# First attention: scores three groups ahead of their exponentials, banks handed out in another order, pieces of work moved between visits

## The chip, the core and the metric

The kernel runs on one core of a Trainium2 chip. The core has five engines, each with its own instruction queue that is worked off in order: TensorE (PE, matmul; PEld is its weight load), VectorE (DVE), ScalarE (ACT), GpSimd (POOL) and SyncE (SP, which issues the DMAs). Matmuls write to PSUM, which has eight banks; a bank of the tiles used here holds 128 partitions of 2 x 256 floats. The metric is the device time of one execution in microseconds (us).

## The reference

A block of four layers, all in float32, on x of 16 batches x 256 tokens x 128 channels: attention a, a gated expert network, attention b, and the expert network again, each after a layer norm and with a residual. The change is in attention a alone. It has 16 heads of 8 channels, and `_binlinear` is a linear layer whose weights are sign(W) times the mean of |W| over a row. Cut to what it computes:

```python
x = x + _L0_attn_a_ref(_layernorm(x, axis=-1), ...)
x = x + _L0_ffn_ref(_layernorm(x, axis=-1), ...)
x = x + _L0_attn_b_ref(_layernorm(x, axis=-1), ...)
x = x + _L0_ffn_ref(_layernorm(x, axis=-1), ...)

def _L0_attn_a_ref(x, Wq, bq, Wk, bk, Wv, bv, Wp, bp):
    q = split_heads(_binlinear(x, Wq, bq))
    k = split_heads(_binlinear(x, Wk, bk))
    v = split_heads(_binlinear(x, Wv, bv))
    att = jnp.einsum('bhtd,bhsd->bhts', q, k) * scale
    att = jax.nn.softmax(att, axis=-1)
    y = jnp.einsum('bhts,bhsd->bhtd', att, v)
    y = y.transpose(0, 2, 1, 3).reshape(B, T, C)
    return _binlinear(y, Wp, bp)
```

## The kernel before

Attention a goes over 16 batches b, and in each over four groups g of four heads; a group has the number G = 4b + g, from 0 to 63. The four heads j of a group lie on partitions 32j to 32j + 31, so their matmuls use different quarters of PE's rows and run side by side.

Each group passes through these steps. `scores` (L395) computes q k' for a head: two matmuls of 256 columns into one bank (a_s), and a DVE reduce of the bank to the negative row maxima (a_nm, L406). `maxima` (L411) turns the maxima with two PE transposes into a bank (a_mx), and DVE adds them to q (a_qa, L421). `exponentials` (L423) computes k q' a second time, transposed and with the maximum taken off through a_qa, into a bank (a_t); ACT takes the exponential (a_pT, L435). `values` (L438) multiplies two groups' probabilities with v, 16 matmuls of 32 columns of weights into half a bank (a_mv), which ACT copies (a_oT, L454).

Around these, each batch has pieces: `channels` (L352) transposes the normalised x to a_xnT; `project` (L359) makes q and k (bank a_pqk), which ACT copies out with the bias (a_qkc, L367), and SP sends to DRAM by one DMA (a_qks) and back by four into the spread layout (a_qk); `project_v` (L381) makes v; `tokens` (L456) transposes the heads (bank a_oq), DVE takes reciprocals and multiplies (a_rs L471, a_y L472); `turn_back` (L478) transposes again and DVE adds a bias (a_yT, L486); `project_out` (L491) makes the output, DVE adds it to x (L498), and `normalise` (L156) runs its statistics on DVE and the rest on POOL; `gate_channels` (L503) and `gate` (L510) make the logits that the expert network needs.

The order is written out by hand: all five engines run in the order of the program. The main loop (L579) goes over i. Its block issues scores of group i and exponentials of group i - 2, in two halves of two heads each; `together` (L520) takes turns between generators, so that PE's matmuls of four heads alternate. After the block `visit(i)` (L554) issues maxima of group i - 1, and the pieces that `table` (L547) gives to s = i mod 4 with a batch offset: first those that share the bank of the maxima, then those with a bank of their own, then those that share the bank of the values; values are issued for two groups at odd s, in visit i for groups i - 3 and i - 2. Project runs one batch ahead.

Every PSUM tile of attention a has one tag with eight buffers, so the banks go round in the order in which the tiles are asked for: s0, s1, t2, t3, s2, s3, t0, t1 in a block (s for scores, t for exponentials, with the head's number), then those of the visit (two or three), then the next block's.

`begin` (L283) is the start: five warming matmuls on zeros, batch 0's normalisation, the weights (`weights` L252 binarises two matrices on DVE and transposes them on PE; `keep` copies them out), and batch 0's q and k straight into the spread layout (L326). The weights of v and p are binarised in steps between these, and their transposes and copies come in visit 2 (L597). The last visits, from i = n + 2 (n = 64), take 20 pieces of the expert network's first matmuls in between (`own_at`, L578).

Of the kernel before, what the change touches and what calls it, by code (L numbers as in the profile page):

```python
# [17 lines left out]
P = 128  # L18
# [59 lines left out]
def hybrid_kernel(ctx: ExitStack, tc: tile.TileContext, io):  # L78
# [115 lines left out]
    def attention_a(place, filling):  # L194
# [4 lines left out]
        with ExitStack() as st:  # L199
# [4 lines left out]

            wT = {}
# [35 lines left out]
            def fills():  # L241

                for n in "qk":
                    wS[n] = pool.tile([P, NG, NJ, 32], F32, tag="sgn", name=f"wS_{n}")
                    nc.gpsimd.memset(wS[n], 0.0)
                for i in range(4):
                    nm = wpool.tile([P, 2, NJ, 32], F32, tag=f"nm{i}", name=f"a_nm{i}")
                    nc.gpsimd.memset(nm, 0.0)
                    nms.append(nm)
                values_tile()  # L250

            def weights(names, w):  # L252

                alpha = small.tile([P, 2], F32, tag="alpha", name=f"alpha_{names}")
                nc.vector.tensor_reduce(
                    alpha, w, AX.X, ALU.add, apply_absolute_value=True
                )
                nc.vector.tensor_scalar(alpha, alpha, 1.0 / C, None, ALU.mult)
                s = pool.tile([P, 2, C], F32, tag="sg", name=f"sgn_{names}")
                nc.vector.tensor_scalar(s, w, 0.0, 1.0, ALU.is_gt, ALU.subtract)  # L260
                nc.vector.scalar_tensor_tensor(s, w, 0.0, s, ALU.is_ge, ALU.add)
                yield

                nc.vector.tensor_tensor(s, s, w, ALU.subtract)
                nc.vector.tensor_tensor(s, s, w, ALU.add)
                yield
                nc.vector.tensor_tensor(
                    s, s, alpha.unsqueeze(2).to_broadcast([P, 2, C]), ALU.mult
                )
                pt = psum.tile([P, 2, T], F32, tag="x", name=f"wT_{names}", bufs=8)[:, :, 0:C]  # L270
                for i in range(2):
                    nc.tensor.transpose(pt[:, i, :], s[:, i, :], ident)
                yield pt
# [9 lines left out]
            def begin():  # L283


                fills()

                warm = psum.tile([P, 2, T], F32, tag="x", name="a_warm", bufs=8)
                for _ in range(5):
                    nc.tensor.matmul(  # L290
                        warm[:, 0], wS["q"][:, 0].rearrange("p j e -> p (j e)"),
                        wS["q"][:, 0:2].rearrange("p g j e -> p (g j e)"),
                        start=True, stop=True,
                    )
# [9 lines left out]
                together(channels(0, half_bank("a_lnT0")))  # L304
                next(qk)
                pt = next(qk)
                nc.vector.tensor_scalar(bq, a_bq, SCALE, None, ALU.mult)
                nc.vector.tensor_scalar(bq_, a_bq_, SCALE, None, ALU.mult)
                xns[1] = normalise(1)
# [6 lines left out]
                keep("qk", pt)  # L316
                vp = weights("vp", a_w[1])
                spread_tile(False)
                to = spread[0]
                q[0], k[0] = to[:, 0], to[:, 1]  # L320
                for half in range(2):
                    for i, (n, bias) in enumerate((("q", bq_), ("k", a_bk_))):
                        pp = psum.tile([P, 2, T], F32, tag="x", name=f"a_p{n}_{half}", bufs=8)
# [6 lines left out]
                        if i:  # L330
                            next(vp)
                        for j in range(2):
                            g = 2 * half + j
                            if i:
# [8 lines left out]
                return vp  # L343
# [5 lines left out]
            def half_bank(name):  # L349
                return psum.tile([P, 2, T], F32, tag="x", name=name, bufs=8)[:, 0]  # L350

            def channels(b, pt):  # L352
                for t in range(2):
                    nc.tensor.transpose(pt[:, t * P : (t + 1) * P], xns[b][:, t, :], ident)
                yield
                xnT[b] = pool.tile([P, T], F32, tag="xnT", name=f"a_xnT{b}")
                nc.scalar.copy(xnT[b], pt)

            def project(b):  # L359

                pp = psum.tile([P, 2, T], F32, tag="x", name=f"a_pqk{b}", bufs=8)
# [10 lines left out]
                to = spread[b % 3]  # L372
# [22 lines left out]
            def scores(G, j):  # L395
# [3 lines left out]
                sc = psum.tile([P, 2, T], F32, tag="x", name=f"a_s{G}_{j}", bufs=8)  # L399
# [23 lines left out]
            def exponentials(G, j):  # L423
# [3 lines left out]
                sc = psum.tile([P, 2, T], F32, tag="x", name=f"a_t{G}_{j}", bufs=8)  # L427
# [28 lines left out]
            def tokens(b):  # L456

                ys[b] = work.tile([P, 2, C], F32, tag="y", name=f"a_y{b}")
                po = psum.tile([P, 2, 2, P], F32, tag="x", name=f"a_oq{b}", bufs=8)
# [18 lines left out]
            def turn_back(b, py):  # L478
# [7 lines left out]
                nc.vector.tensor_scalar(yTs[b], py, a_bv, None, ALU.add)  # L486
# [40 lines left out]
            def of(b):  # L527
                return 0 <= b < NB
# [11 lines left out]
            vp = begin()  # L540
            for i in range(2):
                spread_tile(True)
                values_tile()
            nc.gpsimd.memset(ones, 1.0)
# [3 lines left out]
                ([(project, 1)], [(gate, -3)], []),  # L548
                ([], [(project_out, -2)], []),
                ([(tokens, -1)], [], [(project_v, 1), (channels, 2)]),  # L550
                ([], [(turn_back, -1)], [(gate_channels, -2)]),
            )

            def visit(i):  # L554
                b, s = divmod(i, NG)
                alone, with_maxima, with_values = (
                    [(f, b + d, *r) for f, d, *r in pieces if of(b + d)] for pieces in table[s]
                )
                own_bank = lambda which: psum.tile(
                    [P, 2, T], F32, tag="x", name=f"a_m{which}{i}", bufs=8  # L560
                )
                parts = []
                if 1 <= i < n + 1 or with_maxima:
                    pt = own_bank("x")
                    if 1 <= i < n + 1:
                        parts.append(maxima(i - 1, pt[:, 0]))
                    parts += [f(*r, pt[:, 1]) for f, *r in with_maxima]
                parts += [f(*r) for f, *r in alone]
                pair = s % 2 == 1 and 3 <= i < n + 2
                if pair or with_values:  # L570
                    pt = own_bank("v")
                    parts += [f(*r, pt[:, k]) for k, (f, *r) in enumerate(with_values)]
                    if pair:
                        parts.append(values(i - 3, pt[:, 1]))
# [3 lines left out]
            own_at = {2: 3, 3: 3, 4: 2, 5: 3, 6: 4, 7: 3, 8: 2}  # L578
            for i in range(NG * (NB + 2) + 1):  # L579
                b, s = divmod(i, NG)  # L580
                for half in range(2):
# [3 lines left out]
                    if 2 <= i < n + 2:  # L585
                        parts += [exponentials(i - 2, 2 - 2 * half + j) for j in range(2)]
                    together(*parts)
                    if not i and not half:
                        together(channels(1, half_bank("a_lnT1")))
                if i >= n + 2:  # L590
                    place["h"] = (epool, 5, psum, "x", 8)
                    place["y"] = (psum, "x", 8)
# [3 lines left out]
                if i == 2:  # L596
                    keep("vp", next(vp))  # L597
                    pv = psum.tile([P, 2, T], F32, tag="x", name="a_pv0", bufs=8)
                    together(project_v(0, pv[:, 0]))
                visit(i)  # L600
                if i == 1:
                    xns[2] = normalise(2)
                if i in (5, 9):
                    load_later(i // 9)
                if s == 3 and of(b + 3):
                    xns[b + 3] = normalise(b + 3)
# [423 lines left out]
    def bank(psum, tag, name, bufs):  # L1030

        if tag == "ss":
# [307 lines left out]
```

## Time and profile before

| | us |
|---|---|
| time, median of 3 runs (lowest to highest) | 1552.05 (1549.66 to 1553.44) |
| time of the profiled execution | 1550.1 |
| span of its trace | 1548.3 |
| start of group 0's scores, of group 4's scores | 14.07, 34.29 |
| twelve batches in the middle, each | 17.30 |
| first matmul of the expert network | 299.95 |
| granted PE clock, mean of the span | 0.997 |

The span is what the trace covers, from the first instruction to the last. A row of the windows view gives the length of a stretch, then for PE, PEld, DVE, ACT and POOL the busy time and, in brackets, the number of instructions, then the granted clock of PE as a share of full speed, the busy share of the DMA engines and their GB/s. A row of the timeline gives start, duration, engine, line, operation, output<-inputs and how many instructions were merged; a bracket at its end is idle time before it and what ended that. One float32 matmul stands in PE's rows as two records. Records of PE overlap: a matmul of 256 columns lasts 374 ns in its record, and the next in the same rows starts 216 ns after it.

### The profile page before, as it was taken

How to read it: one execution, taken by the hardware profiler on the slowest of the kernel's cores; microseconds unless marked ns; L12 is line 12 of the kernel's file. 1: busy time of each engine (PE TensorE's matmuls, PEld its weight loads, DVE VectorE, ACT ScalarE, POOL GpSimd, SP SyncE). 2: the span in 40 equal slices, each digit the busy share in tenths (PEclk: the TensorE clock that was granted, in tenths of full speed). 3: DMA queues.
4: the chain of work that ended last, by engine and by line, in shares of the span. 5: the costliest groups of instructions: out<-in, count | busy, mean ns of one | idle time of the engine just before them, and what ended most of it. 6: DMA issues, size and time to landing. Idle time of an engine off the chain costs nothing. (4 is left out here: it accounts for less than half of the span.)

```text
span 1548.3 us, 30874 instructions
## 1 busy us (share of the span) xinstructions
PE 1527.9 (99%) x12284; PEld 860.9 (56%) x12284; DVE 810.3 (52%) x1642; ACT 833.4 (54%) x2074; POOL 403.5 (26%) x518
## 2 busy tenths in 40 slices
PE   8999999999999999999999999999999999999998
PEld 5777777644444444444577777777544444444444
DVE  6888887536133312212599999999363133212122
ACT  3666666544443434343588888888644434344342
POOL 4232323100001000003289888887100000000000
PEclk8999999999999999999999999999999999999999
DMA  3511111000223211111122222222001133211210
GB/s 83 155 32 29 29 36 36 2 8 1 71 64 80 58 38 39 36 41 34 22 57 51 50 48 53 56 54 41 8 1 49 48 79 89 52 48 37 45 41 7
DMA packets 174127, 69.91 MB, mean 45 GB/s; under 512 B 74520, under 2 KB 173600, under 8 KB 173728
## 3 DMA queue, kind: packets, MB, share of 16 engines
q1 hardware_dynamic: 173408, 67.54, 19.1%
q8 instruction: 97, 1.59, 0.4%
q10 hardware_dynamic: 576, 0.41, 0.1%
q14 instruction: 46, 0.38, 0.1%
HBM read 50.88 MB, written 12.58 MB: 41 GB/s over the span
## 5 line engine op out<-in xcount | busy, mean ns | idle before, releaser
L1042 ACT ACTIVATE hT<-ph,head 128x512 f32<-128x512 f32 x512 | 351.2, 687 | 420.9 <-PE ph L1040 418.4
L1040 PE MATMUL ph<-xn,w 128*128 128x512 f32 x1024 | 464.5, 594 | 1.1 <-ACT hT L1042 1.1
L1051 PE MATMUL py<-hT,w 128*128 128x512 f32 (+1 forms) x1040 | 461.3, 586 | 1.0 <-ACT logits L941 0.5
L1051 PEld LDWEIGHTS py<-hT,w 128*128 128x128 f32 x1040 | 196.6, 190 | 237.3 <-issue 230.8
L1040 PEld LDWEIGHTS ph<-xn,w 128*128 128x128 f32 x1024 | 191.3, 190 | 228.0 <-issue 224.2
L1165 DVE SCALAR_TENSOR_TENSOR gy<-py,head,gb 128x512 f32<-128x512 f32 x82 | 61.5, 750 | 425.6 <-PE py L1051 419.3
L855 ACT ACTIVATE b_pr<-b_s,b_nm 128x256 f32<-128x256 f32 x512 | 235.9, 473 | 58.8 <-DVE b_nm L850 58.6
L406 DVE TENSOR_REDUCE a_nm<-a_s 128x2 f32<-128x512 f32 x256 | 160.3, 685 | 52.0 <-PE a_t L429 35.6
L850 DVE TENSOR_REDUCE b_nm<-b_s 128x4 f32<-128x1024 f32 x128 | 152.7, 1193 | 21.5 <-PE b_s L840 21.2
L840 PE MATMUL b_s<-b_kT,b_qd 64*64 64x256 f32 x1024 | 159.9, 382 | 0.2 <-ACT b_pr L855 0.2
L435 ACT ACTIVATE a_pT<-a_t 128x512 f32<-128x512 f32 x256 | 133.2, 598 | 47.2 <-PE a_t L429 46.7
L865 DVE STREAM_TRANSPOSE b_pT<-b_pr 128x1024 f32<-128x1024 f32 x128 | 157.1, 1227 | 0.0
L840 PE MATMUL b_s<-strip,b_qb 64*64 64x256 f32 x2048 | 156.6, 376 | 0.0
L840 PE MATMUL b_s<-b_kS,b_qd 64*64 64x256 f32 x1024 | 156.5, 382 | 0.0
L401 PE MATMUL a_s<-a_qk 32*128 32x256 f32 x1024 | 134.4, 390 | 0.0
L730 POOL TENSOR_TENSOR b_qd<-b_qsel,head 128x512 f32<-128x512 f32 x64 | 84.0, 1335 | 177.6 <-DMA b_qsel<-b_qT 168.9
L152 POOL TENSOR_SCALAR ve<-mv 128x2 f32<-128x2 f32 x64 | 14.6, 229 | 435.1 <-DVE mv L149 429.2
L429 PE MATMUL a_t<-a_qa,a_qk 32*128 32x256 f32 x1024 | 121.9, 394 | 3.5 <-DVE a_qa L421 2.7
L855 ACT ACTIVATION_READ_ACCUMULATOR b_pr<-b_s,b_nm 128x1 f32 x512 | 104.1, 203 | 0.0
L401 PEld LDWEIGHTS a_s<-a_qk 32*128 32x128 f32 x1024 | 91.1, 185 | 22.5 <-issue 15.2
L161 POOL TENSOR_SCALAR xn<-x,mv,rstd 128x128 f32<-128x128 f32 x126 | 99.7, 800 | 6.6
L840 PEld LDWEIGHTS b_s<-strip,b_qb 64*64 64x64 f32 x2048 | 78.3, 133 | 32.2
(176 smaller groups left out, 1439.7 us busy)
## 6 DMA issues: line engine op xcount, KB each, us to landing
gb<-gd SPq DMA_DIRECT2D x128, 256.0 KB
w<-in_w SPq DMA_DIRECT2D x2, 2048.0 KB
a_qks<-a_qkc SPq DMA_DIRECT2D x15, 256.0 KB
a_qk<-a_qks SPq DMA_DIRECT2D x60, 64.0 KB
x<-in_x SPq DMA_DIRECT2D x16, 128.0 KB
b_qs<-b_qT SPq DMA_DIRECT2D x64, 32.0 KB
b_qsel<-b_qT SPq DMA_DIRECT2D x64, 32.0 KB
b_z<-b_qs SPq DMA_DIRECT2D x16, 128.0 KB
```

What stands on the lines that cost most here:

```text
L161: (last or nc.gpsimd).tensor_scalar(xn[:, t, :], xs[b][:, t, :], mv[:, t, 0:1], rstd[:, t : t + 1], ALU.subtract, ALU.mult,)
L401: nc.tensor.matmul(sc[:, t, :], q[b][rows, g, t * P : (t + 1) * P], k[b][rows, g, :], start=True, stop=True,)
L406: nc.vector.tensor_reduce(nms[G % 4][:, :, j, 0:1].rearrange("p t o -> p (t o)"), sc, AX.X, ALU.max, negate=True,)
L429: nc.tensor.matmul(sc[:, t, :], k[b][rows, g, t * P : (t + 1) * P], qaug[G][rows, :], start=True, stop=True,)
L435: nc.scalar.activation(pT, sc, AF.Exp)
L840: nc.tensor.matmul(sc[64 * c : 64 * c + 64, r, u, :], (qb_[rows, at, c] if rel else qd[rows, at, x]).rearrange("p h q -> p (h q)"), strip[ ...
L850: nc.vector.tensor_reduce(nm, sc, AX.X, ALU.max, negate=True)
L855: nc.scalar.activation(pr[:, u, r, :], sc[:, r, u, :], AF.Exp, bias=nm[:, r, u : u + 1], scale=1.0, accum_out=sums[b][:, n : n + 1],)
L865: nc.vector.transpose(pT[:, half % 2, 4 * i : 4 * i + 4].rearrange("p n k h q -> p (n k h q)"), probs.pop(U).rearrange("p u r k -> p (u r ...
L1040: nc.tensor.matmul(ph, w1[:, m * P : (m + 1) * P], xn2[c], start=True, stop=True)
L1042: nc.scalar.activation(hT, ph, AF.Gelu_apprx_tanh, bias=b1[:, m : m + 1], scale=1.0)
L1051: nc.tensor.matmul(py[:, 0:width], w2[:, e * NHC + k, :], hs[k], start=k == 0, stop=k == NHC - 1)
```

## The change

- The main loop starts at i = 3, and its block pairs scores of group i with exponentials of group i - 3. The scores of groups 0 to 2, the first projections and the first maxima move into `begin`, where a group's four heads are issued together (`matmuls`).
- The banks become eight tags of one buffer each, handed out by `bank8` from a ring. After each block the ring is put into the order (2, 0, 3, 1, 6, 4, 7, 5) of the block's tiles: t2, s0, t3, s1, t0, s2, t1, s3.
- The table gives the pieces to other visits: values at even s, for groups i - 4 and i - 3. Project runs two batches ahead (in s = 1), channels three; the spread layout gets a fourth tile, and a_xnT a third buffer.
- a_yT goes from DVE to ACT.
- The start: the warming matmuls use a tile of their own that is zeroed first, and there are nine in three places instead of five; the weights of v and p are transposed in `begin`; three of the four copies of batch 0's q and k go to ACT where two did.

```diff
@@ begin
-                for _ in range(5):
-                    nc.tensor.matmul(
-                        warm[:, 0], wS["q"][:, 0].rearrange("p j e -> p (j e)"),
...
+                warming(6)
                 mv, rstd = statistics(0)
...
+                together(channels(0, bank8("a_lnT0")[:, 0]))
+                warming(2)
                 next(qk)
-                pt = next(qk)
+                next(qk)
                 nc.vector.tensor_scalar(bq, a_bq, SCALE, None, ALU.mult)
                 nc.vector.tensor_scalar(bq_, a_bq_, SCALE, None, ALU.mult)
-                xns[1] = normalise(1)
+                pt = next(qk)
+                warming(1)
...
                 keep("qk", pt)
+                xns[1] = normalise(1)
                 vp = weights("vp", a_w[1])
+                next(vp)
...
-                            if i:
+                            if i and not half:
...
-                return vp
+                next(vp)
+                next(vp)
+                for i in range(2):
+                    spread_tile(True)
+                    values_tile()
+                    if not i:
+                        nc.gpsimd.memset(ones, 1.0)
+                        together(*(scores(0, j) for j in range(NJ)))
+                        second = matmuls(1)
+                        together(channels(1, bank8("a_lnT1")[:, 0]))
+                        keep("vp", next(vp))
+                        xns[2] = normalise(2)
+                        together(maxima(0, bank8("a_mx0")[:, 0]))
+                        together(project(1))
+                        together(*second)
+                third = matmuls(2)
+                pt = bank8("a_mv2")
+                together(project_v(0, pt[:, 0]), channels(2, pt[:, 1]))
+                together(maxima(1, bank8("a_mx1")[:, 0]))
+                together(*third)
+                xns[3] = normalise(3)
+                spread_tile(True)
+
+            def matmuls(G):
+
+                parts = [scores(G, j) for j in range(NJ)]
+                for _ in range(2):
+                    for g in parts:
+                        next(g)
+                return parts
@@ the banks
+            ring = deque(range(8))
+
+            def bank8(name):
+                i = ring.popleft()
+                ring.append(i)
+                return psum.tile([P, 2, T], F32, tag=f"x{i}", name=name, bufs=1)
@@ project, turn_back
-                to = spread[b % 3]
+                to = spread[b % 4]
...
-                nc.vector.tensor_scalar(yTs[b], py, a_bv, None, ALU.add)
+                nc.scalar.activation(yTs[b], py, AF.Identity, bias=a_bv, scale=1.0)
@@ the table (alone, with the maxima's bank, with the values' bank), for s = 0 to 3
             table = (
-                ([(project, 1)], [(gate, -3)], []),
-                ([], [(project_out, -2)], []),
-                ([(tokens, -1)], [], [(project_v, 1), (channels, 2)]),
-                ([], [(turn_back, -1)], [(gate_channels, -2)]),
+                ([], [(gate, -3)], [(turn_back, -2)]),
+                ([(project, 2)], [(project_out, -2)], []),
+                ([], [], [(channels, 3)]),
+                ([(tokens, -1)], [], [(project_v, 2), (gate_channels, -2)]),
             )
+
+            extra = {3: ([(project, 2)], [], [(project_v, 1)]), 4: ([], [], [(channels, 3)])}
@@ the main loop
-                pair = s % 2 == 1 and 3 <= i < n + 2
+                pair = s % 2 == 0 and i < n + 4
...
-                        parts.append(values(i - 3, pt[:, 1]))
+                        parts.append(values(i - 4, pt[:, 1]))
...
-            own_at = {2: 3, 3: 3, 4: 2, 5: 3, 6: 4, 7: 3, 8: 2}
-            for i in range(NG * (NB + 2) + 1):
+            own_at = {3: 3, 4: 3, 5: 4, 6: 4, 7: 4, 8: 2}
+            for i in range(3, NG * (NB + 2) + 1):
...
-                    if 2 <= i < n + 2:
-                        parts += [exponentials(i - 2, 2 - 2 * half + j) for j in range(2)]
+                    if i < n + 3:
+                        parts += [exponentials(i - 3, 2 - 2 * half + j) for j in range(2)]
                     together(*parts)
...
+                if i < n:
+                    used = list(ring)
+                    ring.clear()
+                    ring.extend(used[k] for k in (2, 0, 3, 1, 6, 4, 7, 5))
...
-                if s == 3 and of(b + 3):
-                    xns[b + 3] = normalise(b + 3)
+                if i == 4 or s == 2 and of(b + 4):
+                    xns[b + 3 + (s == 2)] = normalise(b + 3 + (s == 2))
```

## The prediction

> **What bounds the kernel now.** I read the page's busy shares first, then stage windows, the list of waits on TensorE (PE), and last the timeline of one batch in the steady middle.
>
> ```profile
> PE 1527.9 (99%) x12284; PEld 860.9 (56%) x12284; DVE 810.3 (52%) x1642; ACT 833.4 (54%) x2074; POOL 403.5 (26%) x518
> ```
>
> PE is the bound, but its busy time is modelled, and one matmul's record overlaps the next, so 99% does not say that nothing is lost. What is lost shows in the distance between starts. The first attention is the stretch from 14 to about 300 us; the change touches nothing after it.
>
> ```profile
> 10.00:20.00 10.00, 9.78 (x57) 6.53 (x56) 6.61 (x13) 2.89 (x7) 7.48 (x11) 0.87 0.39 111
> 20.00:30.00 10.00, 6.16 (x46) 4.88 (x46) 5.54 (x14) 3.01 (x7) 2.52 (x4) 0.66 0.18 37
> 30.00:40.00 10.00, 9.74 (x136) 6.85 (x136) 7.15 (x16) 6.51 (x15) 3.22 (x5) 1.00 0.04 11
> ```
>
> These windows (length, then busy time and count on PE, weight load, DVE, ACT, POOL, then granted clock) show the start: from 20 to 30 us PE runs 46 instructions where the next window has 136, at a clock of 0.66. The timeline of PE there says why; the bracket is idle time and its releaser:
>
> ```profile
> 19.08 0.70 PE L401 MATMUL a_s<-a_qk 32*128 32x256 f32 x4
> 21.74 0.48 PE L429 MATMUL a_t<-a_qa,a_qk 32*128 32x256 f32 x2 [1.96 <-DVE a_qa L421]
> ...
> 26.17 0.66 PE L272 MATMUL wT_vp<-head,sgn_vp 128*128 128x128 f32 x2 [1.73 <-DVE sgn_vp L267]
> ...
> 29.92 0.48 PE L401 MATMUL a_s<-a_qk 32*128 32x256 f32 x2
> ```
>
> Group 3's scores start only at 29.92, those of group 4 (batch 1) at 34.29.
>
> In the steady middle, twelve batches from 51.08 to 258.69 take 17.30 us each. The four visits of one batch:
>
> ```profile
> 146.22:149.98 3.76, 3.63 (x49) 2.83 (x45) 2.70 (x6) 2.44 (x5) 3.22 (x5) 1.00 0.39 70
> 149.98:154.89 4.91, 4.91 (x72) 3.43 (x71) 4.66 (x13) 2.74 (x6) 0.00 (x0) 1.00 0.01 3
> 154.89:158.51 3.62, 3.62 (x47) 2.85 (x43) 2.53 (x6) 2.71 (x6) 2.53 (x4) 1.00 0.00 0
> 158.51:163.52 5.01, 5.01 (x72) 3.45 (x71) 4.24 (x13) 2.93 (x6) 0.00 (x0) 1.00 0.26 81
> ```
>
> And the first of them in the timeline of all engines:
>
> ```profile
> 146.22 0.48 PE L401 MATMUL a_s<-a_qk 32*128 32x256 f32 x2
> ...
> 147.38 2.48 DVE L406 TENSOR_REDUCE a_nm<-a_s 128x2 f32<-128x512 f32 x4 [1.06 <-PE a_t L429]
> 147.47 2.06 ACT L435 ACTIVATE a_pT<-a_t 128x512 f32<-128x512 f32 x4 [0.74 <-PE a_t L429]
> 148.16 0.44 PE L415 MATMUL a_mx<-head,a_nm 128*128 128x128 f32 x2
> 148.73 0.65 PE L462 MATMUL a_oq<-head,a_oT 128*128 128x128 f32 x4
> 149.78 0.41 DVE L421 TENSOR_TENSOR a_qa<-a_qk,a_mx 128x256 f32<-128x256 f32 x1
> 149.98 0.48 PE L401 MATMUL a_s<-a_qk 32*128 32x256 f32 x2
> 150.25 0.48 PE L429 MATMUL a_t<-a_qa,a_qk 32*128 32x256 f32 x2
> 150.49 0.42 DVE L472 TENSOR_TENSOR a_y<-a_oq,a_rs 128x256 f32<-128x256 f32 x1
> ```
>
> A block (scores of one group, exponentials of another) takes 146.22 to 148.16 = 1.94 us unhindered. The waits are hidden inside "busy": (a) 148.16 to 148.73 = 0.57 where two transposes need 0.27 (the second starts 0.165 after the first, the next 0.11 later); L462 waits for a bank that DVE's second reduce frees at 148.67, and refilling costs 0.06 more: 0.36. (b) The block at 149.98 ends at 152.22, 2.24 instead of 1.94: first the exponentials start 0.27 after the scores (waiting for a_qa), later one of them, at 151.07, waits for the bank of a_oq, which L472 empties at 150.92: 0.30. (c) The third visit has none. (d) The block at 158.51 ends at 160.84, 2.33: 0.40, again a_qa. Sum 1.06, so a batch without waits would be 17.30 - 1.06 = 16.24 us.
>
> **The change, part by part, in the steady middle.** No matmul is added or taken away there; pieces change visits. Without waits the new visits would take: s=0: the old fourth visit, 5.01 - 0.40 = 4.61, minus project_out (4 x 0.111) plus gate (0.365) plus turn_back (2 x 0.109): 4.76. s=1: the old third, 3.62, minus gate plus project_out: 3.70. s=2: the old second, 4.91 - 0.30 = 4.61, minus turn_back and gate_channels (4 x 0.109) plus channels (2 x 0.109): 4.39. s=3: the old first, 3.40. Sum 16.25, the same.
>
> The wait on a_qa is gone: exponentials of group i-3 use an a_qa made a whole visit earlier. What replaces it follows from the bank order (2,0,3,1,6,4,7,5): after a block the banks go out as t2, s0, t3, s1, t0, s2, t1, s3 and then this visit's own. Offsets from a block's start, from the timeline above: reduces s0 to s3 end at 1.85, 2.45, 3.05, 3.65 (1.16 + 0.60 each, last tail 0.085), ACT empties t2, t3, t0, t1 at 1.85, 2.33, 2.82, 3.31, a_qa ends at 3.97, L472 at 4.70; a PE instruction starts 0.06 to 0.11 after its releaser. The next block's second half starts at its own 0.97.
> - s=3: a_mx takes t2's bank (1.85, needed 1.94: no wait), a_oq takes t3's: 2.33 + 0.06 = 2.39, needed 1.94 + 0.27 = 2.21; 0.18, with refilling 0.24. The visit becomes 3.64.
> - s=0: the last exponential of the second half takes a_oq's bank: 4.70 + 0.11 = 4.81, needed 3.64 + 0.97 + 0.02 = 4.63: 0.19.
> - s=1: everything free in time (a_mv is emptied 0.51 after the block's start, needed 0.97). Here DVE has its fullest visit: reduces to 3.65, a_qa, the residual add 0.42, statistics 0.72, 4.7 in all against 3.70; it hands 0.2 us to the next visit, whose first reduce could start at 1.16.
> - s=2: the last exponential takes the bank of a_pqk, whose two evacuations end 0.95 after the block's start plus 0.11, needed 0.99: 0.07. The values' second group needs the last exponential's evacuation at 3.31 + 0.1, and gets there at 2.53 + 0.89 = 3.42: 0 to 0.07, I take 0.07.
>
> Sum 0.57 against 1.06: 0.49 us a batch, over 14 batches (the twelve, and one at either end by estimate) 6.9 us. Bounds: nothing (the waits only move), and 14 x 1.06 = 14.8 (all gone).
>
> a_yT moves from DVE (0.48, L486) to ACT (Identity with a bias of that shape: 0.47, L367). Both have room: DVE's work in a batch is 16 x 0.60 of reduces, 4 x 0.33 to 0.41 of a_qa, and about 3 of statistics, adds and tokens, 14 in 16.8; ACT's busy time in the four windows is 10.8. Nothing on PE. Projections two batches ahead: the same five DMAs per batch; their DVE and PE waits in SP's queue are for a tile last read three visits before, behind them stand only the next batch's. Nothing. The later load of w1 stands behind batch 3's projection DMAs: needed seven visits later. Nothing.
>
> **The start.** Nine warming matmuls stand in time where PE waits for DVE anyway (until 6.23, 7.75 and 8.5): nothing. With wS one DVE step of statistics earlier (8.2) and at full clock, the eight projections (each 0.43 then; from 8.76 to 14.0 before, at half clock from 9.24) end near 12.0. From there DVE's row sets the pace: reduces of group 0 from 13.3 to 15.75, statistics 0.7, a_qa 0.41 after the transposes, reduces of group 1 to 19.3; group 2's scores wait for group 1's banks and end at 20.3; projections of v, transposes, a_mx to 21.3; a_qa 21.8, reduces to 24.2, statistics to 24.9, group 3's to 27.3. PE's visit 3 has its scores waiting for the reduces of group 2 to 24.2, ends its block at 25.2, and its pieces (two transposes, project, two project_v: 2.3) at 27.5. Batch 1's q and k come earlier (a_qks near 18.2; before, 18.60, and DMA quiet by 24.5), so group 4 starts at 27.5 against 34.29: 6.8. Left to do then is more: exponentials of group 1 (alone at the end, 1.09 as at 293.29), values (1.87), less project 0.95 and project_v 0.45: 1.6. Gain 5.2. Bounds: 3.2 if the clock drops again, as it did after the idle 19.8 to 21.7, over a window of 6.8 us in which some 4 us of matmul take half as long again; 7.2 if visit 3's pieces hide in its waits.
>
> The Trainium skill (TensorE: Matmul & The Clock Gate, What's actually happening) says that the clock is half or full and is set by windows of 3.41 us of activity. The windows' 0.66 from 20 to 30 us, 6.8 us at half, agrees. By that rule alone the stretch at half clock is worth at most 3.4 us; it is inside my term.
>
> **Sum.** 6.9 + 5.2 = 12.1, the end of the attention taken as even (its fill of 20 units is the same). From the profiled run: span 1548.3 becomes 1536.2, its time 1550.1 becomes 1538.0. The median shown, 1552.05, lies 1.95 higher: 1540.
>
> **Rivals.**
> 1. The steady waits only move (a_oq's bank is the hand-off that remains, in the trace at 151.07 too): gain 5.2, 1547. Against: the parts of a_qa, 0.27 and 0.40, have a whole visit of slack afterwards. 16%.
> 2. All waits vanish: 14.8 + 5.2 = 20, 1532. Against: 4.81 against 4.63 in s=0. 12%.
> 3. The start gives little, since DVE's row is serial there (reduces for four groups, 9.6 us, come before group 4 in either kernel): 6.9 and 0 to 2, 1544. 12%.
> 4. Slower: the evacuation loop closes. A block's first reduce is ready at 1.16, four reduces, a_qa and the hand-off give 4.1, minus 0.97: no visit can be shorter than 3.1, plus what DVE does between; in s=3 that is 3.9 with tokens, in s=1 3.5 with the residual add against 3.70. If DVE's backlog of s=1 passes 0.5 us, s=2 and s=3 wait too; once the waits pass 0.36 in every visit (1.43 a batch, 0.37 over today's, times 14) the start's 5.2 is eaten; at 0.45 a visit, 1.8 a batch, it is 14 x 0.74 - 5.2 = +5, 1557. For it: DVE is 95% busy in the second visit above. 7%. The Trainium skill (TensorEngine Tiling (Array Packing), PSUM Bottleneck) says that tiling speeds up PE and not the evacuation, which may then bound; here DVE's 14 of 16.8 us says not yet.
>
> **Chances.** The forecast 53%. Its own range is 1536 to 1544. For 8 in 10 I reach to rivals 2, 1 and 3: 1530 to 1549. A difference under 0.3% (4.7 us) can't be told from none: the forecast, rival 2 and nearly all of rival 3 are faster by more, rival 1 lies on the edge and is split: faster 0.85, same 0.08, slower 0.07.
>
> **What would show it.** A batch of 16.8 us, exponentials starting with their scores in every block (no 0.27), L503 (a_oq) 0.45 after the first a_mx; group 4's scores at 27 to 28 us; granted clock above 0.9 from 10 to 20. A batch of 17.2 or more, or group 4 after 32, makes me wrong.

## The result and the profile after

| | before | after |
|---|---|---|
| time, median of 4 runs each, taken alternately on one chip (lowest to highest), us | 1550.86 (1549.57 to 1553.44) | 1540.24 (1539.13 to 1541.12) |
| ratio, with 95% interval | | 0.9929 (0.9912 to 0.9946) |
| time of the profiled execution, its span, us | 1550.1, 1548.3 | 1539.13, 1537.3 |

The change makes the kernel 10.6 us faster (0.7%), to 1540.24 us, where 1540 us had been predicted. Read from the starts of the scores and of the first expert matmul in both traces, the 11.0 us between the spans lie here:

| stretch, us | before | after | difference | predicted |
|---|---|---|---|---|
| start of the span to group 4's scores | 34.29 | 29.57 | -4.72 | -6.8 |
| group 4 to group 56, 13 batches | 224.40 | 217.23 | -7.17 | -6.4, for 13 of its 14 batches |
| group 56 to the first expert matmul | 41.26 | 42.82 | +1.56 | +1.1: +1.6, less 0.49 for the 14th batch |
| the rest of the span, untouched | 1248.3 | 1247.7 | -0.6 | 0 |

The busy shares of the page say as little as before:

```profile
PE 1524.0 (99%) x12292; PEld 858.5 (56%) x12292; DVE 800.1 (52%) x1624; ACT 838.7 (55%) x2092; POOL 405.9 (26%) x521
```

PE is still 99% busy by its records. Of the 11.0 us, 3.9 come out of its busy time (1527.9 to 1524.0) and 7.1 out of its idle time (20.4 to 13.3). The windows view of the changed kernel's start (length; busy time and count on PE, weight load, DVE, ACT, POOL; granted clock; DMA share; GB/s):

```profile
10.00:20.00 10.00, 8.81 (x68) 6.04 (x67) 8.46 (x19) 3.84 (x11) 8.70 (x13) 1.00 0.40 116
20.00:30.00 10.00, 9.35 (x68) 6.83 (x67) 6.22 (x14) 3.93 (x9) 6.60 (x10) 0.83 0.17 29
30.00:40.00 10.00, 10.00 (x146) 7.24 (x142) 7.92 (x17) 7.61 (x18) 2.52 (x4) 1.00 0.32 80
```

From 10 to 20 us the clock is full (0.87 before). From 20 to 30 it is 0.83: the clock's records show half speed from 24.82 to 28.24. The same view of one steady batch, visit by visit (s = 2, 3, 0, 1):

```profile
154.63:159.14 4.51, 4.51 (x70) 3.07 (x69) 4.48 (x14) 2.90 (x6) 2.52 (x4) 1.00 0.21 71
159.14:162.78 3.64, 3.63 (x49) 2.84 (x45) 2.66 (x7) 2.71 (x6) 3.18 (x5) 1.00 0.37 58
162.78:167.80 5.02, 5.02 (x73) 3.51 (x72) 3.92 (x10) 2.72 (x6) 0.03 (x1) 1.00 0.02 3
167.80:171.47 3.67, 3.67 (x47) 2.92 (x43) 2.50 (x5) 2.80 (x6) 0.00 (x0) 1.00 0.00 0
```

A batch takes 16.84 us (17.30 before). The timeline from the end of s = 3 into s = 0:

```profile
161.08 0.44 PE L456 MATMUL a_mx<-head,a_nm 128*128 128x128 f32 x2
161.53 0.66 PE L503 MATMUL a_oq<-head,a_oT 128*128 128x128 f32 x4
...
162.78 0.48 PE L442 MATMUL a_s<-a_qk 32*128 32x256 f32 x2
162.79 0.48 PE L470 MATMUL a_t<-a_qa,a_qk 32*128 32x256 f32 x2
...
163.41 0.42 DVE L513 TENSOR_TENSOR a_y<-a_oq,a_rs 128x256 f32<-128x256 f32 x1
...
163.90 0.48 PE L470 MATMUL a_t<-a_qa,a_qk 32*128 32x256 f32 x2
```

The two waits that were forecast are both there. a_oq starts 0.45 after a_mx where 0.27 is the bare distance: it waits for t3's bank, which the bank order gives it. In the next block, exponentials start with their scores (162.79 after 162.78), but a later one starts at 163.90, right behind a_y's end at 163.84, since it gets a_oq's bank.

### The profile page after: what moved, and what is told of

The parts are those of the page before. It is cut to its first block, busy times and chain, and to the rows that moved or that the text cites. A ratio compares the mean times of both kernels' runs of the same rounds, so it can differ in the third digit from the quotient of the medians.

```text
span 1537.3 us, 30882 instructions
## 1 busy us (share of the span) xinstructions
PE 1524.0 (99%) x12292; PEld 858.5 (56%) x12292; DVE 800.1 (52%) x1624; ACT 838.7 (55%) x2092; POOL 405.9 (26%) x521
## 5 line engine op out<-in xcount | busy, mean ns | idle before, releaser
L470 PE MATMUL a_t<-a_qa,a_qk 32*128 32x256 f32 x1024 | 134.5, 394 | 0.7 <-DVE a_nm L447 0.6
L442 PE MATMUL a_s<-a_qk 32*128 32x256 f32 x1024 | 130.3, 390 | 0.4 <-DVE a_nm L447 0.4
L470 PEld LDWEIGHTS a_t<-a_qa,a_qk 32*128 32x128 f32 x1024 | 100.1, 185 | 4.8 <-issue 1.7
```

The costliest lines, as they stand in the source:

```text
L442: nc.tensor.matmul(sc[:, t, :], q[b][rows, g, t * P : (t + 1) * P], k[b][rows, g, :], start=True, stop=True,)
L470: nc.tensor.matmul(sc[:, t, :], k[b][rows, g, t * P : (t + 1) * P], qaug[G][rows, :], start=True, stop=True,)
```

## The experiments

Each kernel is the changed one with the edit shown; times are medians, and each ratio is against runs of the kernel before on the same chip. The sets were run on several chips, and the median of the kernel before is 1550.86 to 1552.63 us in them, so a difference of 2 us between two rows of times says little by itself; the distances inside the profiles say more. "Group 4" is the start of its scores.

| edit | time, us | ratio (95%) | steady batch | group 4 | half clock in the first 50 us of the profile |
|---|---|---|---|---|---|
| none | 1540.24 | 0.9929 (0.9912 to 0.9946) | 16.84 | 29.57 | 3.4 us |
| exponentials two groups behind | 1546.72 | 0.9972 (0.9962 to 0.9981) | 17.30 | 29.43 | none |
| ring not reordered | 1546.54 | 0.9967 (0.9954 to 0.9980) | 17.24 | 31.38 | 10.2 us |
| another bank for a_oq | 1540.73 | 0.9926 (0.9911 to 0.9941) | 16.84 | 31.37 | 10.2 us |
| group 2's maxima first | 1538.22 | 0.9912 (0.9897 to 0.9927) | 16.83 | 28.76 | 6.8 us |
| a_yT on DVE | 1542.60 | 0.9935 (0.9919 to 0.9952) | 17.00 | 31.00 | 10.2 us |
| three warmings less | 1542.44 | 0.9934 (0.9919 to 0.9948) | 16.84 | 33.03 | 3.4 and 10.2 us |
| maxima first, four warmings more | 1536.36 | 0.9898 (0.9883 to 0.9912) | 16.84 | 26.14 | none |
| tokens in s = 0 | 1535.86 | 0.9893 (0.9878 to 0.9908) | 16.50 | 29.60 | 3.4 us |
| projections one batch ahead | 1544.25 | 0.9948 (0.9930 to 0.9966) | 16.84 to 17.91 | 28.57 | 6.8 us |
| maxima, warmings and tokens | 1532.71 | 0.9872 (0.9856 to 0.9888) | 16.50 | 26.17 | none |
| four warmings more alone | 1538.81 | 0.9911 (0.9894 to 0.9927) | 16.84 | 29.05 | 3.4 us |

### The steady batch: lag, ring, a_oq's bank

**Exponentials two groups behind**, as before the change:

```diff
-                together(*third)
+                together(*third, *(exponentials(0, j) for j in range(NJ)))
...
-                    if i < n + 3:
-                        parts += [exponentials(i - 3, 2 - 2 * half + j) for j in range(2)]
+                    if i < n + 2:
+                        parts += [exponentials(i - 2, 2 - 2 * half + j) for j in range(2)]
```

> The changed kernel with exponentials two groups behind the scores again (group 0's are issued at the end of the start); bank order, table and all else stay. My theory (the lag takes the wait on a_qa away): in the blocks that follow the two short visits, s=3 and s=1, a_qa ends 3.97 us after the earlier block's start, so the exponentials start 0.40 after the scores; s=0 takes 5.16 (a_oq's wait is swallowed), s=2 takes 4.84, a batch 17.3 instead of 16.84, the time about +6 us on the changed kernel, 1546. Rival (the bank order made the gain, the lag nothing): a batch stays at 16.84, time 1540.

Measured: 17.30 us a batch. The visits s = 2 and s = 0 in its windows view:

```profile
158.23:163.07 4.84, 4.84 (x70) 3.28 (x69) 4.65 (x15) 2.93 (x6) 2.59 (x5) 1.00 0.23 75
...
166.71:171.87 5.16, 5.16 (x73) 3.62 (x72) 3.98 (x10) 2.74 (x6) 0.00 (x0) 1.00 0.01 3
```

Only these two are longer (4.84 against 4.51, 5.16 against 5.02; s = 3 and s = 1 take 3.64 and 3.67), and in their blocks the timeline has the exponentials 0.46 and 0.39 us after the scores, the first of them here:

```profile
158.23 0.70 PE L442 MATMUL a_s<-a_qk 32*128 32x256 f32 x4
158.69 0.48 PE L470 MATMUL a_t<-a_qa,a_qk 32*128 32x256 f32 x2
```

That is the wait on a_qa of the kernel before. With the new ring and the new dealing but the old lag, all of the batch's gain is gone: without the lag the new ring and the new dealing are worth nothing here.

**The ring in the order in which the banks were used**, which takes the permutation out:

```diff
-                    ring.extend(used[k] for k in (2, 0, 3, 1, 6, 4, 7, 5))
+                    ring.extend(used)
```

> The changed kernel with the banks handed out simply in turn. My theory, worked out from when each bank is emptied: s=3 loses its 0.24 (a_oq now takes t2's bank), but s=0 waits 0.35 for s3's bank and 0.07 for a_oq's, s=1 to s=2 0.05 and 0.07, and the bank of the values in s=2 costs 0.30: 0.9 of waits a batch instead of 0.57, 17.15, about +4 us, 1544. Rival (the order of the banks does not matter, only the lag does): 16.84, 1540.

Measured: 17.24, with 3.66, 4.91, 3.41 and 5.26 for s = 1, 2, 3, 0; the time of 1546.54 is 2.5 above the one expected, and its profile has 10.2 us at half clock in the start. The order of the ring is worth 0.40 us a batch, and the lag without it next to nothing: 17.24 against the old 17.30. The two parts need each other. Both runs keep the new dealing of the pieces; what lag and ring would give without it was not tried.

**Another bank for a_oq**, s0's in place of t3's:

```diff
-                    ring.extend(used[k] for k in (2, 0, 3, 1, 6, 4, 7, 5))
+                    ring.extend(used[k] for k in ((2, 3, 0, 1, 6, 4, 7, 5) if s == 3 else (2, 0, 3, 1, 6, 4, 7, 5)))
```

> The changed kernel with one other bank order after blocks of s=3: t2, t3, s0, s1, ..., so that a_oq takes s0's bank (empty at 1.85) instead of t3's (2.33). My theory (what ends s=3 and s=0 is DVE's row: a_oq is emptied 4.70 us after the block's start, however early PE wrote it): s=3 falls from 3.64 to 3.40, s=0 rises by as much from 5.03 to 5.27, a batch stays at 16.84 within 0.05, time 1540. Rival (each wait costs by itself): 16.60 a batch, 3.4 us less, 1537.

Measured: s = 3 3.41 and s = 0 5.26, the batch 16.84 as before. This one wait does move: the 0.23 us that a_oq no longer waits, the exponential in the next block waits longer, because a_y empties a_oq's bank at DVE's own time, and that had not become earlier.

**Tokens a visit later**, in s = 0, where DVE has time for a_y before the bank is asked for; other pieces are dealt anew round it, and the loop runs seven visits longer, with the expert network's pieces spread over them:

```diff
-                ([], [(gate, -3)], [(turn_back, -2)]),
-                ([(project, 2)], [(project_out, -2)], []),
-                ([], [], [(channels, 3)]),
-                ([(tokens, -1)], [], [(project_v, 2), (gate_channels, -2)]),
+                ([(tokens, -2)], [], [(gate_channels, -4)]),
+                ([(project, 2)], [(project_out, -3)], []),
+                ([], [(turn_back, -2)], [(channels, 3)]),
+                ([], [(gate, -4)], [(project_v, 2)]),
...
-                    ring.extend(used[k] for k in (2, 0, 3, 1, 6, 4, 7, 5))
+                    ring.extend(used[k] for k in ((2, 0, 3, 1, 6, 4, 7, 5) if s else (2, 3, 0, 1, 6, 4, 7, 5)))
```

> In the steady batch the tokens' transpose (a_oq) moves from the block of s=3 to that of s=0, a batch later, with a_t and the rest dealt anew round it. By my theory of the waits, a_oq then no longer waits for t3's bank and the last exponential of s=0 no longer for a_oq's bank: visits 3.70, 4.68, 3.29 and 4.83 for s=1, 2, 3, 0, batch 16.50 instead of 16.84, 13 batches, 4.4 us less, of which the longer tail takes 1 to 2 back: 1537 (1536 to 1538). Rival, the waits only move, as they did when a_oq got another bank: batch 16.84, and with the longer tail 1541 to 1542.

Measured: 1535.86 us, 16.50 a batch. Its windows, s = 2, 3, 0, 1:

```profile
151.40:156.12 4.72, 4.72 (x71) 3.25 (x70) 4.69 (x16) 3.38 (x7) 3.02 (x5) 1.00 0.19 61
156.12:159.32 3.20, 3.20 (x46) 2.69 (x42) 2.04 (x5) 2.60 (x6) 2.69 (x5) 1.00 0.45 73
159.32:164.28 4.96, 4.96 (x74) 3.48 (x73) 4.36 (x10) 2.56 (x6) 0.00 (x0) 1.00 0.06 9
164.28:167.90 3.62, 3.62 (x47) 2.84 (x43) 2.46 (x5) 2.71 (x6) 0.00 (x0) 1.00 0.00 0
```

The sum is as forecast to 0.01 us, the visits one by one only to 0.13 (s = 0 forecast at 4.83, measured 4.96). So 0.34 of the 0.59 us that a batch of 16.84 lies above the prediction's sum without waits (16.25) can be had without a new bank or a matmul less, by what is asked for where. The time came out just below the range expected (1536 to 1538). The longer tail is there: from the first expert matmul to the end the span takes 1250.6 us, against 1247.7 in the changed kernel.

### Two parts that the prediction had put at nothing

**a_yT back on DVE**:

```diff
-                nc.scalar.activation(yTs[b], py, AF.Identity, bias=a_bv, scale=1.0)
+                nc.vector.tensor_scalar(yTs[b], py, a_bv, None, ALU.add)
```

> The copy of a_yT (one per batch, 0.48 us on ScalarE in the changed kernel) goes back to VectorE, where it was before the change; all else stays changed. My theory: in a steady batch of 16.84 us neither engine is the one that is waited for where this copy stands, so the batch stays 16.84 (within 0.05) and the time 1540 (1539 to 1541). Rival, VectorE sets the pace of the steady batch (it ends most of the long waits: a_mx 0.8 us and a_t 0.6 us of the waits' list): 0.48 us more work on it per batch shows in full, batch 17.3, 14 batches, time 1546 to 1547.

Measured: neither. The batch is 17.00, all of the 0.16 in s = 1. The timeline of that block, first in the changed kernel, then with a_yT on DVE:

```profile
167.94 0.47 ACT L527 ACTIVATE a_yT<-a_mv,head 128x256 f32<-128x256 f32 x1 [1.85 <-PE a_mv L486]
...
168.31 0.36 ACT L495 COPY a_oT<-a_mv 128x256 f32<-128x256 f32 x1
```

```profile
187.47 0.48 DVE L527 TENSOR_SCALAR a_yT<-a_mv,head 128x256 f32<-128x256 f32 x1 [1.10 <-PE a_mv L486]
...
187.99 0.37 ACT L495 COPY a_oT<-a_mv 128x256 f32<-128x256 f32 x1 [2.37 <-DVE a_yT L527]
...
188.41 0.48 PE L470 MATMUL a_t<-a_qa,a_qk 32*128 32x256 f32 x2
```

a_yT and a_oT read the two halves of one bank. On two engines the copy a_oT starts only after a_yT is done (187.99, released by a_yT), and the bank is free 1.03 us after the block's start at 187.33; the exponential that gets it starts at 188.41. On one engine the second starts 0.10 before the first ends, and the bank is free 0.87 after the block's start at 167.80. PE wants it at about 0.97. Not the load on DVE but the hand-over between two readers of a bank decides here: 0.16 us a batch, about 2 us in all. The times fit with that (1542.60 against 1540.24) but do not settle it by themselves, as the intervals of the ratios overlap; the distance of the visits does.

**Projections one batch ahead**: the table's project, channels and project_v a batch later, the two extra visits' pieces left out; the normalisation comes a batch later too.

```diff
-                ([(project, 2)], [(project_out, -2)], []),
-                ([], [], [(channels, 3)]),
-                ([(tokens, -1)], [], [(project_v, 2), (gate_channels, -2)]),
+                ([(project, 1)], [(project_out, -2)], []),
+                ([], [], [(channels, 2)]),
+                ([(tokens, -1)], [], [(project_v, 1), (gate_channels, -2)]),
...
-            extra = {3: ([(project, 2)], [], [(project_v, 1)]), 4: ([], [], [(channels, 3)])}
+            extra = {}
```

> The projections go back to one batch ahead (project, channels and project_v each a batch later, the two extra visits' pieces left out); their places in the visit stay. My theory: the steady batch does not feel it. The second set of a batch's DMAs is over some 7 us after the projection's last copy (in the trace copy at 172.42, DMAs busy until 178.4), and the scores would want it 1.2 us later than that (179.6). Batch 16.84; group 4 up to 1.3 us earlier (two pieces fewer in visit 3), which the last batches give back as 1.3 to 1.5 us of projections at the end: 1540 (1539 to 1541). Rival, the two batches are needed because the round trip through memory is not done in time: scores of s=0 wait, batch 17.3 or more, time 1546 or more.

Measured: 1544.25; the expectation fails in its middle and holds at its ends. Group 4 comes 1.0 us earlier, and from group 56 to the first expert matmul it takes 44.28 us, 1.46 more. But between group 4 and group 56 it loses 3.6 us, all of it in s = 0: most batches take 16.84, but the three from group 8 to group 20 lose 0.7 to 0.8 each (during the first two the expert network's weights are loaded too), and one later batch takes 17.91. Here is that one: the DMA issues in the timeline of SP, then PE's timeline in the block of s = 0.

```profile
156.80 0.38 SPq L412 DMA_DIRECT2D a_qks<-a_qkc  x1
160.16 1.32 SPq L416 DMA_DIRECT2D a_qk<-a_qks  x4
```

```profile
163.97 0.79 PE L442 MATMUL a_s<-a_qk 32*128 32x256 f32 x3
...
165.03 0.37 PE L442 MATMUL a_s<-a_qk 32*128 32x256 f32 x1
...
165.32 1.13 PE L442 MATMUL a_s<-a_qk 32*128 32x256 f32 x3
```

The first DMA takes 3.36 us until the second set is issued (2.2 to 2.3 in most batches), and the transfers are busy until 164.27 by their records, 7.47 after the first issue. The block wants the tile 7.17 after it. The margin was read as 1.2 us from one batch of one trace; by the records of the transfers it is 0.5 to 0.8 in most batches (round trips of 6.4 to 6.7), and in three (7.4 to 7.9) below nothing. That the lone scores wait for this tile is inferred from these times; the trace names no releaser there. The records do not give the whole margin either: the batch at 61.42 waits as well, though its own transfers end at 61.19. Two batches ahead is thus not without use: where project now stands, in s = 1 and no longer in s = 0, one batch ahead is too late, by about 4 us in all.

### The start: order and clock

**Group 2's maxima first**: the reduces of group 2 go ahead of group 1's a_qa on DVE.

```diff
-                together(maxima(1, bank8("a_mx1")[:, 0]))
                 together(*third)
+                together(maxima(1, bank8("a_mx1")[:, 0]))
```

> The changed kernel with group 2's reduces ahead of group 1's a_qa in the start (DVE waited for a_mx from 19.2 to 21.7 there while group 2's scores lay ready at 20.3). My theory (DVE's row sets the pace of the start): the reduces come 1.5 us earlier, group 4 starts at 27 to 28 us instead of 29.57, and PE's clock may not drop in the window from 24.8 us; time 1.5 to 3 us less, 1537 to 1538.7. Rival (batch 1's q and k or PE itself set the pace there): group 4 at 29.5, time 1540.

Measured: 1538.22, group 2's reduces 1.9 us earlier (20.1 against 22.0), group 4 at 28.76 and not at 27 to 28; but the clock in its profile was at half for 6.8 us, twice as long as in the changed kernel's. By the ratios the time can't be told from the changed kernel's (0.9912 and 0.9929, with overlapping intervals); the reduces can.

**Three warming matmuls less**, the two and the one among the first transposes; the six ahead of them stay:

```diff
-                warming(2)
...
-                warming(1)
```

> The three warming matmuls that the changed kernel puts among the first transposes (two, then one) are taken out; the six ahead of everything stay. My theory: they are what kept the granted clock at 1.00 from 10 to 20 us, so the clock is at half again for some 3.4 us around 9 to 13, the first projections end 1.5 to 2 us later (at 13 to 14 instead of 11.6) and the time is 1541.5 to 1542. Rival, the first projections came earlier because of the order alone (VectorE and the copies set the pace there, not the clock): projections still end by 12 and the time is 1540.

Measured: scores of group 0 at 13.76, 1.6 later than with them. The granted clock of the first 10 us by the windows view is 0.92 (1.00 with them). The first projections in the timeline, first in the changed kernel, then here:

```profile
8.54 1.10 PE L343 MATMUL a_pq<-a_xnT,wS_q 128*128 128x256 f32 x4
```

```profile
8.55 2.05 PE L341 MATMUL a_pq<-a_xnT,wS_q 128*128 128x256 f32 x4 [0.48 <-DVE wS_q L324]
```

The clock is at half from 8.37 to 11.78, and the same four instructions take 2.05 us that took 1.10. So 1.6 of the 1.9 us by which group 0's scores come earlier than in the kernel before (12.16 against 14.07) are the clock's, not the order's. What the other edits of the start are worth, one by one, was not tried. The time, 1542.44, can't be told from the changed kernel's by the ratios (0.9934 and 0.9929, with overlapping intervals); the shift of the scores can.

**Maxima first, and four warming matmuls more**, one after the first v transposes and three ahead of group 2's scores, where PE waits for DVE:

```diff
...
+                        warming(1, lnT1[:, 1])
                         xns[2] = normalise(2)
...
                         together(project(1))
+                        warming(3, mx0[:, 1])
                         together(*second)
...
-                together(maxima(1, bank8("a_mx1")[:, 0]))
                 together(*third)
+                together(maxima(1, bank8("a_mx1")[:, 0]))
```

> Group 2's maxima come ahead of group 1's transposed maxima, as in the run that gave 1538.2, and four warming matmuls are added in gaps where TensorE waits anyway (one after the first values are projected, three ahead of group 2's scores), each into the unused half of a bank. My theory: the clock fell between 20 and 30 us because TensorE's activity was sparse there; with the gaps filled it stays at 1.00 from 5 to 40 us, group 4's scores start at 27 to 27.5 us (28.8 without the warming), and the runs lie close together at 1536 (1535.5 to 1536.5). Rival, the drop is not due to these gaps (the 4-row matmuls themselves are what counts as idle, or it is set by the chip): a half-clock window of 3.4 us or two stays between 20 and 30, group 4 at 28.5 to 29, and the time is 1538 to 1540, in two groups.

Measured: 1536.36 (1535.99 to 1537.29), group 4 at 26.14. In the windows view:

```profile
20.00:30.00 10.00, 10.00 (x122) 7.78 (x121) 8.82 (x19) 6.40 (x14) 6.57 (x10) 1.00 0.29 66
```

122 PE instructions from 20 to 30 us where the changed kernel has 68, and the clock full throughout.

**The four warmings alone**, to part the clock from the order: the edit above without its last two lines of maxima and `third`.

> The four warming matmuls in the gaps of the start alone; the maxima of group 1 and 2 keep the changed kernel's order. My theory: of the 3.4 us that group 4 came earlier with both edits (26.14 against 29.57), the clock and the order each have their own part. The order put group 2's reduces 1.9 us earlier (20.1 against 22.0), and VectorE's row hands some 1.9 us of that on; the clock alone then gives 1.5: group 4 at 28.1 (27.6 to 28.5), clock 1.00 from 5 to 40 us, time 1538.6 (1538 to 1539.3). Rival, the clock is all of it: group 4 at 26.1 to 26.6 and 1536.4; or nothing of it, since VectorE sets the pace in the start: group 4 at 29 to 29.6 and 1540.

Measured: 1538.81 (1537.78 to 1541.15). In the profile the clock did fall, from 23.61 to 27.02, with group 4 at 29.05, so the expectation of a full clock failed there, though not that of the time. Two of the four runs report a mean clock of 1.000, at 1537.8 and 1537.9; the others have 0.999 and 0.998, at 1539.7 and 1541.2. With the old order there is another gap (PE waits 0.65 us for group 2's reduces, until 22.80), which the warmings do not cover. Whether this gap made the clock fall is not shown: with group 2's maxima first, and no warmings, PE has no such gap and the clock fell earlier still, at 20.04. By the ratios the time can't be told from the changed kernel's (0.9911 and 0.9929). The two runs at full clock lie 1.5 us above the median with the order as well (1536.36): an estimate for the changed kernel's group 4 at full clock is then 26.14 + 1.5 = 27.6.

**Maxima, warmings and tokens together**, the two edits shown above in one kernel:

> Group 2's maxima first, the four warming matmuls in the gaps of the start, and the tokens moved to s=0, together. My theory: the parts are in different stages and add up, 3.9 us from the start (1536.4 against 1540.2) and 4.4 from the batch (1535.9 against 1540.2): 1532 (1531 to 1533.5), batch 16.50, group 4 at 26.1. Rival, one of the gains is not its own: the steady batch of 16.50 needs two batches to settle from the start's backlog, or part of the 4.4 was luck with the clock's windows; then 1534 to 1536.

Measured: 1532.71 (1531.78 to 1533.65), ratio 0.9872, the fastest of all: 7.5 us less than the changed kernel, 8.3 by the sum of the two parts' gains. Batch 16.50 and group 4 at 26.17, so both parts are there in full, and the first expert matmul comes 9.3 us earlier than in the changed kernel (280.29 against 289.62); 3.7 us of that are lost behind it. The kernel with the tokens alone loses 2.9 there, since its attention ends later behind the first expert matmul; the rest comes with another window at half clock (below).

## Why the prediction was right, and where it was not

**The steady term: right, by its mechanism.** Predicted 16.8 a batch, measured 16.84; the gain is 0.47 in each of the ten batches in the middle and 0.65 and 0.61 in the two beside them, 5.93 over the twelve where 5.9 was forecast. The visits were forecast at 3.70, 4.53, 3.64 and 4.95 for s = 1, 2, 3, 0 and are 3.67, 4.51, 3.64 and 5.02. a_oq's wait for t3's bank is there (0.45 after a_mx, as written), and so is the exponential behind a_y, where s = 0 loses 0.26 in place of 0.19. With the old lag the batch is 17.30, with the plain ring 17.24: rival 1, that the steady waits only move, falls for the change as a whole; for a_oq's bank it holds, as the run with another bank shows. Rival 2 falls: 0.59 us of waits are left over 16.25. Rival 4 falls: no wait spreads to every visit. Of the two batches that the term adds at the ends, the one from group 4 to 8 gave more, 1.24; the other lies behind group 56.

**The start: the step was over-sized, 4.7 in place of 6.8.** Group 4 starts at 29.57, neither at 27 to 28 nor after 32. The prediction named a clock that drops again as its lower bound, 3.2 for start and end together, and took its sum at full clock as the value; measured are 4.72 less 1.56, 3.16 (with the 14th batch's gain in it), so the start came out at its bound. The clock did drop, for one window of 3.41 us, from 24.82 to 28.24, while visit 3's pieces ran:

```profile
27.20 1.06 PE L404 MATMUL a_pqk<-a_xnT,wq 128*128 128x256 f32 x2
28.06 0.69 PE L404 MATMUL a_pqk<-a_xnT,wk 128*128 128x256 f32 x2
```

The first pair, q, took 1.06 at half clock; at full clock such a pair takes 0.60 (at 16.14). A window of 3.41 us at half can cost 1.7 us at most, and 27.6 by the estimate above plus 1.7 is 29.3: by this estimate up to 1.7 of the 2.1 us is the clock, 0.3 stays unassigned, and the hand sum along DVE's row (27.5) was about right. Rival 3, that the start gives little, falls. Every start here has its half clock in stretches of 3.4, 6.8 or 10.2 us, or none, and nothing between. The Trainium skill (TensorE: Matmul & The Clock Gate, What's actually happening) says that the clock is half or full and is set by windows of 3.41 us; the traces agree.

**The end: near.** "Left to do then is more: 1.6" stands beside a 14th batch that gives 0.49, and both lie behind group 56: +1.1 together, measured +1.56.

**The two edits put at nothing.** The sum was not hurt, since the kernel as changed shows no wait from either, but the reasons given were not the ones that count. For a_yT the text looked at the engines' load; and "a_mv is emptied 0.51 after the block's start" was wrong: it is 0.87, and 0.97 is when PE wants it. For the projections it named what stands behind the DMAs, not how long the round trip is against the time until the scores.

**The median.** 1.95 us were added to go from a profiled run to the median. The terms gave 12.1 where 11.0 came, so the profiled run came out 1.1 above the forecast (1539.13 against 1538.0); but it lay only 1.1 below its median, not 1.95. The two misses nearly cancel in the forecast's 1540, which is luck. The gain itself is 10.6 by the medians, as the kernel before had 1550.86 in these runs, not 1552.05. A miss of 2 us in the start was inside the stated range.

## What to carry to other kernels

- Where PE's records show it always busy, measure the distance between the starts of equal blocks and take from it the same block without waits; write down for each bank when it is emptied and when it is next asked for. That list gave 0.49 us a batch where 0.47 came, and a better dealing than the change's own (16.50) after it.
- A longer lag between producer and consumer gains only if the banks are handed out in the order in which they come free: on top of the new dealing, either alone was worth 0.06 us or less of the 0.46 a batch.
- Before putting a moved copy or transfer at nothing, ask when its result or its bank is wanted, and by how much it is early, in the tightest of the batches and not in one; an engine's load does not tell that.

## What the runs showed of the hardware

- The half-clock stretch in the start varied from profile to profile by whole windows in kernels whose first 20 us are the same: 3.4 us in the changed kernel, 10.2 with another bank for a_oq, 10.2 with a_yT on DVE. Group 4 moved with it, from 29.57 to 31.37. Only the profiles with four more warmings and group 2's maxima first, and the one with the lag of two, had none; other runs of the last report a mean clock down to 0.995. No long pause of PE stands ahead of such a fall: from 9 us to the fall at 24.82 PE's longest idle time in the changed kernel is 0.76 us by its records, and 0.76 us up to the fall at 20.04 with maxima first. What in PE's work decides it was not tried. The profiled runs of the changed kernel and of the one with another bank (1539.13 and 1540.82) differ by 1.7 us and their group 4 by 1.8, so a part of the scatter of some 2 us between runs of one kernel can be the clock in the start: the changed kernel's four runs are 1539.13 and 1539.37 at a mean clock of 0.999, and 1541.11 and 1541.12 at 0.997.
- In three profiles (maxima first; warmings alone; maxima, warmings and tokens) another window at half clock stood near 740 us, where the changed kernel has none. In the first two the stretch from the first expert network's search (its first compare on DVE) to the end took 1219.5 and 1219.8 us, against 1217.3 in the changed kernel; in the third it took 1219.0, against 1218.2 with the tokens alone. Why it falls there in some runs was not tried.
- The round trip of a 256 KB tile through memory, by the records of its transfers, took 6.4 to 7.1 us in most batches, and 7.4, 7.5 and 7.9 in three (issued at 71.90, 156.80 and 242.22 with projections one batch ahead) in which no other transfer shows; until the second set was issued it took 2.2 to 2.3 us in most, 3.2 to 3.5 in these three. Such batches are no matter of that edit: the kernel before has them at 142.18 and 228.68 (7.6 and 8.2), the changed one at 71.44 (8.3).
